# Four layers on 16 images: layers 2 and 3 of one pair of images issued in steps between the tap streams of the next pair, and score rows by ScalarE alone

## The chip, the core and the metric

The kernel runs on one core of a Trainium2 chip. Five engines have each their own queue of instructions: PE (TensorE, matrix products), DVE (VectorE), ACT (ScalarE), POOL (GpSimd) and SP (SyncE, which issues DMAs). The metric is the device time of one execution in microseconds (us), taken as a median of several runs. A profile is one more execution with a hardware record of every instruction; its span goes from the first to the last instruction.

## The reference, cut to what matters

The input x is 16 images of 128 channels and 28 x 28 pixels, in fp32. Four layers follow one another.

```python
# layer 0: group normalization, then x + L1 distances of every 3x3 patch to 128 filters
neg_l1 = -sum(abs(W[f, k] - patch[k]))           # k over 128 channels x 9 taps
# layer 1: two 3x3 convolutions, 4-bit weights, two of nine taps masked; result in 16 levels
out = act_quant(bn(conv(act_quant(bn(conv(x, wq1))), wq2)) + x)
# layer 2, over 784 tokens of 128 channels, on layer-normalized tokens:
Wi = B @ W.T
scores[i, j] = sum_d v[d] * tanh(Wi[j, d] + Wi[i, d])
C = softmax(scores) @ B                          # then 2 of 8 experts for each token
# layer 3: linear attention with elu(.)+1 and a causal mask, then a spectral layer:
# 16 filters, plus and minus, causal convolution over the tokens and a 128x128 mix of each
```

Each layer adds its result to its input. The dear ones are layer 0 (128 x 9 taps of |w - x| over a whole image) and the scores (784 x 784 tanh of 128 channels, of which the symmetric half is computed).

## The kernel before, in words

The kernel has two phases, `conv_layers` (layers 0 and 1, in 8 pairs of images) and `token_layers` (layers 2 and 3, image by image). The levels of all images are kept on chip between them.

**Phase one.** Channels lie on the partitions, and a pair of images is one tile `pad` of 128 x 60 x 30. For each filter and tap one instruction makes a tile `d` of 128 x 1568: ACT takes |x - w| (L312), or DVE takes max(x, w) (L314). |w - x| is 2 max(x, w) - x - w, so a maximum needs the plain tap subtracted, which a matmul with ones does for all filters at once (L304), and a constant `sw`. A second maximum can be added into the same `d` by one more DVE instruction (L316), which saves a tile for PE. PE sums `d` over the channels (L321): a matmul with a column of `sel` into 32 output columns, four filters side by side, in four chunks of 392 pixels. A "stream" is four tiles, one for each quarter of the filters; `in_turn` lays out 264 streams for a pair, with turns that mix ACT tiles and DVE tiles. After each stream one step of `rest` is issued: the quantized convolutions of the pair before, then the group normalization of the pair after. `d` has 16 buffers, `pad` two. At the end of a pair DVE writes `x1p` (L330).

**Phase two.** For every block of 112 tokens, `scores` makes 15 units. DVE adds a column of `wi` to a row of 394 tokens, eight rows to a unit (L709), ACT takes the tanh of the whole tile (L710, 3152 elements), and PE sums over the channels with `vz` (L685), one unit later. `written` moves a block's scores into `sc` after the next block's last unit. After each unit, `tick` issues steps of three generators at fractional rates: `attend` of the image before, then `head` of the next image and experts, linear attention and `normed` of the one before, and `spectral` of the image two before. A spectral job is four matmuls of `up` with a band (L978), a copy by ACT (L984), and a mix into an accumulator (L956); a band is fetched by DMA for two jobs (L963), and the mixing matrices stay on chip. PSUM has two banks for scores, two for accumulators and four that all other steps rotate through. The weights of the spectral layer and its bands are prepared in the steps of image 0.

PE's instructions are kept in the order in which they are written (`in_traced_order`); the other engines' order is set by the tile scheduler near to the written one. Every queue is in order.

Of the kernel before, what the change touches and what calls it, by code (L numbers as in the profile page):

```python
# [9 lines left out]
U8 = mybir.dt.uint8  # L10
# [13 lines left out]
MAX_TAPS, EITHER = [1, 3, 4, 5, 7], 8  # L24
COMMON = [("a", (0,)), ("m", (4,)), ("a", (2,)), ("m", (5,)), ("a", (6,)), ("m", (7,)), ("a", (8,)), ("m", (1, 3))]
FOURTH = [("a", (0,)), ("m", (4,)), ("m", (1,)), ("a", (2,)), ("m", (5,)), ("m", (3,)), ("a", (6,)), ("m", (7,)), ("m", (8,))]


def in_turn():


    quarters = []
    for j, turn in enumerate((0, 2, 5, 7)):
        mine = [(m, *x) for m in range(32) for x in (FOURTH if (m + j) % 4 == 3 else COMMON)]
        quarters.append(mine[turn:] + mine[:turn])
    return list(zip(*quarters))


STREAMS = in_turn()
# [18 lines left out]
class Steps:  # L58


    def __init__(self, *gens, rate=1.0):
        self.gens = [g for g in gens if g is not None]
        self.rate, self.due = rate, 0.0

    def step(self, n=1):
        while n and self.gens:
            try:
                next(self.gens[0])
                n -= 1
            except StopIteration:  # L70
                self.gens.pop(0)

    def tick(self):
        self.due += self.rate
        while self.due >= 1.0:
            self.due -= 1.0
            self.step()

    def each(self):
        while self.gens:  # L80
            self.step()
            yield

    def drain(self):
        while self.gens:
            self.step()
# [8 lines left out]
def rows_of(ap, n):  # L95

    return ap.unsqueeze(0).to_broadcast([n, ap.shape[0]])

# [15 lines left out]
@with_exitstack  # L114
def kernel(ctx: ExitStack, tc: tile.TileContext, a: dict, out: bass.AP):
    nc = tc.nc
    keep = ctx.enter_context(tc.tile_pool(name="keep", bufs=1))

    ident = keep.tile([P, P], F32, name="ident")
    make_identity(nc, ident)  # L120
    ones = keep.tile([P, P], F32, name="ones")
    nc.vector.memset(ones, 1.0)
    mhalf = keep.tile([P, NK], F32, name="mhalf")
    nc.vector.memset(mhalf, -0.5)

    levels = keep.tile([P, B, T], U8, name="levels")

    conv_layers(tc, a, levels, ident, ones, mhalf)
    token_layers(tc, a, out, levels, ident, ones, mhalf)
    in_traced_order(tc, (mybir.EngineType.PE,))  # L130


def rsqrt(nc, out, x, eps, mhalf):

    nc.vector.tensor_scalar(out, x, eps, None, ALU.add)
    nc.gpsimd.tensor_tensor(out, out, mhalf, ALU.pow)  # L136

@with_exitstack  # L140
def conv_layers(ctx, tc, a, levels, ident, ones, mhalf):
    nc = tc.nc
    const = ctx.enter_context(tc.tile_pool(name="a_const", bufs=1))
    xpool = ctx.enter_context(tc.tile_pool(name="a_x", bufs=2))
    small = ctx.enter_context(tc.tile_pool(name="a_small", bufs=2))
    ring = ctx.enter_context(tc.tile_pool(name="a_ring", bufs=16))
    ypool = ctx.enter_context(tc.tile_pool(name="a_y", bufs=3))
    psacc = ctx.enter_context(tc.tile_pool(name="a_acc", bufs=1, space=PSUM))
    psm = ctx.enter_context(tc.tile_pool(name="a_psm", bufs=4, space=PSUM))
    NP = B // 2  # L150

    def load_x(p):
        x = xpool.tile([P, 2, T], F32, tag="x", name=f"x{p}")
        nc.sync.dma_start(x, a["x"][2 * p : 2 * p + 2].rearrange("b c t -> c b t"))
        return x

    xs = {0: load_x(0)}
    w0 = const.tile([P, 9, P], F32, name="w0")
    nc.scalar.dma_start(w0, a["L0_conv_W"])
    wq = {}  # L160
    for name in ("L1_conv_w1", "L1_conv_w2"):
        wq[name] = const.tile([P, 9, P], F32, name=name)
        nc.scalar.dma_start(wq[name], a[name])
# [21 lines left out]
    pads = [const.tile([P, PR, PC], F32, name=f"pad{i}") for i in range(2)]  # L185
    x1p = const.tile([P, PR, PC], F32, name="x1p")
    q1p = const.tile([P, PR, PC], F32, name="q1p")
    for t in (*pads, x1p, q1p):
        nc.vector.memset(t, 0.0)

    nw0 = const.tile([P, 9, P], F32, name="nw0")
    nc.scalar.mul(nw0, w0, -1.0)
# [5 lines left out]
    background = [(k, ones) for k in MAX_TAPS] + [(EITHER, fourth)]  # L198

    wsum = const.tile([P, P], F32, name="wsum")  # L200
    nc.vector.tensor_tensor(wsum, w0[:, EITHER, :], fourth, ALU.mult)
    for k in MAX_TAPS:
        nc.vector.tensor_tensor(wsum, wsum, w0[:, k, :], ALU.add)
    sw_ps = psm.tile([P, 512], F32, tag="psm", name="sw_ps")
    nc.tensor.matmul(sw_ps[:, :1], wsum, ones[:, :1], start=True, stop=True)
    sw = const.tile([P, 1], F32, name="sw")
    nc.vector.tensor_copy(sw, sw_ps[:, :1])

    def quantized_weights():

        for name, w in wq.items():
            nc.scalar.activation(w, w, AF.Tanh)
            yield
            mx = small.tile([P, 1], F32, tag="mx", name="mx_" + name)
            nc.vector.tensor_reduce(mx, w.rearrange("p k f -> p (k f)"), AX.X, ALU.max, apply_absolute_value=True)
            mall = small.tile([P, 1], F32, tag="mall", name="mall_" + name)
            nc.gpsimd.partition_all_reduce(mall, mx, P, bass_isa.ReduceOp.max)
            for _ in range(8):
                yield
            nc.vector.tensor_scalar(mall, mall, 2.0, None, ALU.mult)  # L220
            nc.vector.reciprocal(mx, mall)
            yield
# [4 lines left out]
            yield  # L227


    bn = {}  # L230

    def norms():
        for i, unit in ((0, NLEV), (1, NLEV * NLEV)):
# [3 lines left out]
            for _ in range(4):  # L237
                yield
# [6 lines left out]
            yield  # L245
# [13 lines left out]


    def group_norm(p, lag):
        x, pad = xs[p], pads[p % 2]
        stats = small.tile([P, 2, 2, 6], F32, tag="stats", name=f"stats{p}")
        mv = small.tile([P, 2, 2], F32, tag="mv", name=f"mv{p}")
        for im in range(2):
            for h in range(2):
                nc.vector.bn_stats(stats[:, im, h, :], x[:, im, h * NCK : (h + 1) * NCK])
            nc.vector.bn_aggr(mv[:, im, :], stats[:, im])
            yield
        ps = psm.tile([P, 512], F32, tag="psm", name=f"gm_ps{p}")  # L270
        nc.tensor.matmul(ps[:, :2], grp, mv[:, :, 0], start=True, stop=True)
        for _ in range(lag):
            yield
        gm = small.tile([P, 2], F32, tag="gm", name=f"gm{p}")
        nc.vector.tensor_copy(gm, ps[:, :2])
        dev = small.tile([P, 2], F32, tag="dev", name=f"dev{p}")
# [3 lines left out]
        yield  # L280
        ps = psm.tile([P, 512], F32, tag="psm", name=f"gv_ps{p}")
        nc.tensor.matmul(ps[:, :2], grp, dev, start=True, stop=True)
        for _ in range(lag):
            yield
        rstd = small.tile([P, 2], F32, tag="rstd", name=f"rstd{p}")
        rsqrt(nc, rstd, ps[:, :2], 1e-5, mhalf[:, :2])
        for _ in range(lag):
            yield
        for im in range(2):
# [4 lines left out]
            yield  # L294

    def l1_distances(p, rest):


        pad = pads[p % 2]
        accs = [psacc.tile([P, 512], F32, tag=f"acc{c}", name=f"acc{p}_{c}") for c in range(4)]  # L300

        for i, (k, of) in enumerate(background):
            for c in range(4):
                nc.tensor.matmul(accs[c][:, :NCK], of, window(pad, k, 14 * c, 14), start=i == 0, stop=False)  # L304
        for n, stream in enumerate(STREAMS):
            made = []
            for j, (m, kind, taps) in enumerate(stream):
                f = 32 * j + m
                d = ring.tile([P, 2 * HW, HW], F32, tag="d", name=f"d{p}_{f}_{taps[0]}")
                k = taps[0]  # L310
                if kind == "a":
                    nc.scalar.activation(d, window(pad, k, 0, 2 * HW), AF.Abs, bias=nw0[:, k, f : f + 1])  # L312
                else:
                    nc.vector.tensor_scalar(d, window(pad, k, 0, 2 * HW), w0[:, k, f : f + 1], None, ALU.max)  # L314
                    for k in taps[1:]:
                        nc.vector.scalar_tensor_tensor(  # L316
                            d, window(pad, k, 0, 2 * HW), w0[:, k, f : f + 1], d, ALU.max, ALU.add)
                made.append(d)
            for c in range(4):
                for j, (m, kind, _) in enumerate(stream):  # L320
                    nc.tensor.matmul(  # L321
                        accs[c][32 * j : 32 * j + 32, :NCK], sel[kind][:, 31 - m : 63 - m],
                        made[j][:, 14 * c : 14 * c + 14, :], start=False, stop=n == len(STREAMS) - 1,
                    )
# [723 lines left out]
```

## Time and profile before

| | us |
|---|---|
| median of 3 runs (12472.03 to 12472.23) | 12472.12 |
| profiled execution, its own time | 12472.97 |
| its span | 12470.9 |
| PE busy | 11890.7 (95%) |
| DVE busy | 11408.4 (91%) |
| ACT busy | 10934.1 (88%) |
| phase one, start to the last `x1p` | 0 to 6191 |
| between the phases and image 0 | 6191 to 6753 |
| images with all three generators | 6753 to 11521 |
| the last 366 us, after image 15's scores | 12105 to 12471 |

In the list of groups a line shows the line of the kernel, the engine, the operation, what it writes and reads with partitions x elements, the count, then the total busy time and the mean ns of one, and last the idle time of the engine just before them with what ended it. A matmul in fp32 has two records. Instructions of one engine overlap a little, so a mean is longer than the distance from one start to the next. In a timeline, a line is a start, a length and how many instructions of a group follow each other.

### The profile page before, as it was taken

Reading aid. Unit: us, or ns where it says so; the run is one execution under the profiler, and the core shown is the slowest. Engines: PE = TensorE matmul, PEld = TensorE weight load, DVE = VectorE, ACT = ScalarE, POOL = GpSimd, SP = SyncE. Lnnn points to the kernel's source line nnn. Section 1 sums busy time; section 2 is a strip of 40 time slices with the busy share of each in tenths; the row PEclk is TensorE's granted clock in tenths of the full one; section 3 lists DMA queues with packets and bytes.
Section 4 is the critical chain, followed back from the end, with each engine's and each line's share of the span. In section 5 each row is a group of like instructions: output and inputs, shape, how many; then the busy total and the mean of one; then the engine's idle time right before and its main releaser. Section 6 shows DMA issues by size and latency. Waiting matters only on the chain.

```text
span 12470.9 us, 260867 instructions
## 1 busy us (share of the span) xinstructions
PE 11890.7 (95%) x109746; PEld 5640.7 (45%) x109746; DVE 11408.4 (91%) x23240; ACT 10934.1 (88%) x7253; POOL 294.4 (2%) x129
## 2 busy tenths in 40 slices
PE   9999999999999999999956899999999999999999
PEld 4444444444444444444412444454444454444456
DVE  9989989899998999989989999999999999999982
ACT  8989989899898999989878888888888888888872
POOL 0000000000000000000010000000000000000000
PEclk9999999999999999999989999999999999999999
DMA  0000000000000000000020000000000000000001
GB/s 12 2 4 2 4 1 2 4 2 4 2 2 4 2 4 2 2 1 2 3 75 1 13 19 20 20 20 20 20 20 19 20 20 20 20 19 20 19 24 36
DMA packets 111864, 156.91 MB, mean 13 GB/s; under 512 B 13096, under 2 KB 106208, under 8 KB 110688
## 3 DMA queue, kind: packets, MB, share of 16 engines
q1 hardware_dynamic: 110256, 138.46, 4.1%
q8 instruction: 860, 14.09, 0.5%
q14 instruction: 316, 2.59, 0.1%
q10 hardware_dynamic: 432, 1.77, 0.0%
HBM read 127.34 MB, written 12.85 MB: 11 GB/s over the span
## 4 chain that ended last, share of the span: by engine, by line
PE 57%; DVE 32%; issue 5%; ACT 4%; POOL 1%; DMA 0%; SPq 0%; DVEq 0%; POOLq 0%; ACTq 0%
DVE d L314 19%; PE acc L321 17%; PE sp L685 14%; PE u L978 11%; DVE d L316 5%; DVE th L709 5%; PE acc L956 5%; ACT th L710 3%; PE conv_ps L338 2%; PE av L772 2%; PE ex L843 1%; PE acc L304 1%; ACT d L312 1%; PE acc L947 1%; POOL rs_l L136 1%
## 5 line engine op out<-in xcount | busy, mean ns | idle before, releaser
L312 ACT ACTIVATE d<-pad,nw 128x1568 f32<-128x1568 f32 x3840 | 5781.3, 1622 | 214.6 <-PE acc L321 200.8
L321 PE MATMUL acc<-d,sel_m 128*32 128x392 f32 x36864 | 5148.7, 493 | 66.1 <-DVE d L316 57.2
L710 ACT ACTIVATE th<-th 128x3152 f32<-128x3152 f32 (+1 forms) x1680 | 4475.5, 2688 | 431.7 <-DVE th L709 372.9
L321 PE MATMUL acc<-d,sel_a 128*32 128x392 f32 x30720 | 4737.9, 493 | 21.4 <-ACT d L312 20.5
L709 DVE TENSOR_SCALAR th<-wi 128x394 f32<-128x394 f32 (+1 forms) x12544 | 4437.3, 419 | 244.8 <-PE sp L685 219.5
L314 DVE TENSOR_SCALAR d<-pad,w 128x1568 f32<-128x1568 f32 x4608 | 4430.9, 1029 | 80.6 <-PE acc L321 80.1
L685 PE MATMUL sp<-th,vz 128*32 128x394 f32 (+1 forms) x25088 | 2440.7, 509 | 395.5 <-ACT th L710 395.3
L321 PEld LDWEIGHTS acc<-d,sel_m 128*32 128x32 f32 x36864 | 1980.9, 110 | 1745.2 <-issue 1260.4
L321 PEld LDWEIGHTS acc<-d,sel_a 128*32 128x32 f32 x30720 | 1755.6, 110 | 1522.0 <-issue 1269.9
L978 PE MATMUL u<-band,up 128*128 128x392 f32 (+3 forms) x8192 | 1711.2, 349 | 0.0
L978 PEld LDWEIGHTS u<-band,up 128*128 128x128 f32 x8192 | 1342.4, 190 | 773.0 <-PE sp L685 158.5
L685 PEld LDWEIGHTS sp<-th,vz 128*32 128x32 f32 x25088 | 664.0, 110 | 1833.8 <-issue 797.9
L316 DVE SCALAR_TENSOR_TENSOR d<-pad,w,d 128x1568 f32<-128x1568 f32 x768 | 1417.9, 1846 | 8.7
L984 ACT COPY u<-u 128x392 f32<-128x392 f32 x1024 | 493.1, 482 | 518.6 <-PE u L978 518.4
L956 PE MATMUL acc<-u,m_even 128*128 128x392 f32 x1024 | 463.2, 534 | 0.0
L956 PE MATMUL acc<-u,m_odd 128*128 128x392 f32 (+1 forms) x1024 | 461.7, 533 | 0.0
L849 DVE SCALAR_TENSOR_TENSOR t<-ex,gate,t 128x128 f32<-128x128 f32 x896 | 306.8, 343 | 11.9 <-PE ex L843 10.4
L843 PE MATMUL ex<-ew,xt 128*128 128x512 f32 x448 | 213.9, 600 | 0.4 <-DVE t L849 0.4
L772 PEld LDWEIGHTS av<-n,sc 128*128 128x128 f32 x1568 | 181.8, 191 | 50.1 <-issue 28.2
L772 PE MATMUL av<-n,sc 128*128 128x129 f32 x1568 | 196.2, 279 | 0.0
L956 PEld LDWEIGHTS acc<-u,m_odd 128*128 128x128 f32 x1024 | 155.7, 192 | 10.9 <-issue 10.1
L992 DVE TENSOR_TENSOR y<-acc,mask 128x392 f32<-128x392 f32 x32 | 19.0, 594 | 151.5 <-PE acc L956 151.5
(247 smaller groups left out, 4184.3 us busy)
## 6 DMA issues: line engine op xcount, KB each, us to landing
band<-band SPq DMA_DIRECT2D x512, 196.0 KB
x<-in_x_dram SPq DMA_DIRECT2D x8, 784.0 KB
band<-band_out SPq DMA_DIRECT2D x32, 196.0 KB
out_dram<-y SPq DMA_DIRECT2D x16, 392.0 KB
band_in<-in_L_ffn_phi_dram SPq DMA_DIRECT2D x16, 300.1 KB
m_plus<-in_L_ffn_M_phi_plus_dram SPq DMA_DIRECT2D x32, 128.0 KB
m_minus<-n_L_ffn_M_phi_minus_dram SPq DMA_DIRECT2D x32, 128.0 KB
band_in<-in_L_ffn_phi_dram SPq DMA_DIRECT2D x16, 84.8 KB
```

Of the source, the lines that this page charges most:

```text
L312: nc.scalar.activation(d, window(pad, k, 0, 2 * HW), AF.Abs, bias=nw0[:, k, f : f + 1])
L314: nc.vector.tensor_scalar(d, window(pad, k, 0, 2 * HW), w0[:, k, f : f + 1], None, ALU.max)
L316: nc.vector.scalar_tensor_tensor(d, window(pad, k, 0, 2 * HW), w0[:, k, f : f + 1], d, ALU.max, ALU.add)
L321: nc.tensor.matmul(accs[c][32 * j : 32 * j + 32, :NCK], sel[kind][:, 31 - m : 63 - m], made[j][:, 14 * c : 14 * c + 14, :], start=False, s ...
L685: nc.tensor.matmul(sp[32 * j : 32 * j + 32, lo : lo + w], vz[:, 31 - m : 63 - m], th[:, 4 * k + j, :], start=m == 0, stop=m == Q - 1, skip ...
L709: nc.vector.tensor_scalar(th[:, 4 * k + j, :], wi[:, lo : lo + w], wi[:, i : i + 1], None, ALU.add)
L710: nc.scalar.activation(th, th, AF.Tanh)
L772: nc.tensor.matmul(q[:, i * (P + 1) : (i + 1) * (P + 1)], blk(sc[:, k, :], i0 + i), n1[:, k, :], start=k == 0, stop=k == NT - 1)
L843: nc.tensor.matmul(qs[h], blk(xt, i), ew[:, 4 * h : 4 * h + 4, :], start=True, stop=True)
L956: nc.tensor.matmul(acc[to][:, lag:TH], (m_odd if odd else m_even)[:, k, :], u[:, : TH - lag], start=False, stop=k == NK - 1 and odd == 1)
L978: nc.tensor.matmul(q[:, P * i : TH], up[:, jobs[n][2], i, :], t[:, :w], start=i == 0, stop=i == 3)
L984: nc.scalar.copy(u, held_[n - 1][0][:, :TH])
```

## The change

One set of pools and one loop take the place of the two phases.

- Pair 0 keeps the old taps (`ALONE`, 264 streams). Pairs 1 to 7 use `BESIDE`: 208 streams, more merged second taps on DVE, fewer taps on ACT, seven plain taps.
- Between the streams of pair p, three lanes issue steps: the convolutions of pair p-1, the chain (head, attend, experts, linear attention, normed) and the spectral jobs. A step is of kind `EV` (ACT, DVE, POOL) or `PE`; in a stream the EV steps come ahead of the sums and the PE steps behind them.
- Score units come at two a stream (L689): each of a unit's four rows is one ACT tanh with the column as bias. After the last pair (`alone`) DVE adds and ACT takes the tanh of four rows at once (L682, L684).
- `d` tiles have 10 buffers, rows 14; there is one `pad`. PSUM has four banks for the taps, and one each for scores, spectral output, the chain (`psx`) and jobs with convolutions (`psu`).
- Mixing matrices, quantized convolution weights, expert weights and x for the residual are fetched again by DMA when they are needed. Weights and bands are prepared in pair 0.

```diff
+ALONE = Plan(
+    "alone", [tiles("a:0", "m:4", "a:2", "m:5", "a:6", "m:7", "a:8", "m:13")] * 3
+    + [tiles("a:0", "m:4", "m:1", "a:2", "m:5", "m:3", "a:6", "m:7", "m:8")], (0, 2, 5, 7),
+    [(1, "all"), (3, "all"), (4, "all"), (5, "all"), (7, "all"), (8, "fourth")])
+BESIDE = Plan(
+    "beside", [tiles("m:13", "a:0", "m:45", "m:6", "a:2", "m:78")] * 2
+    + [tiles("m:13", "a:0", "m:7", "m:45", "a:2", "m:8", "m:6"),
+       tiles("m:13", "a:0", "m:7", "a:2", "m:45", "a:6", "m:8")], (0, 2, 4, 5),
+    [(1, "all"), (3, "all"), (4, "all"), (5, "all"), (7, "all"), (8, "all"), (6, "rest")])
+RING, ROWS = 10, 14
+RATE_X, RATE_Y, RATE_S, RATE_C, RATE_A, RATE_0 = 1.2, 0.85, 2.0, 1.0, 1.5, 1.2
...
+class Lane:
+    def run(self, turn):
+        while self.gens:
+            if self.turn is None:
+                self.turn = next(self.gens[0], None)
+                if self.turn is None:
+                    self.gens.pop(0)
+            elif self.turn != turn or (turn == PE and self.other and self.other.holds):
+                return False
+            else:
+                self.turn = next(self.gens[0], None)
+                self.holds = turn == PE
+                if self.turn is None:
+                    self.gens.pop(0)
+                return True
+        return False
...
-                        nc.vector.tensor_scalar(th[:, 4 * k + j, :], wi[:, lo : lo + w], wi[:, i : i + 1], None, ALU.add)
-                nc.scalar.activation(th, th, AF.Tanh)
+                    rows = [rows_pool.tile([P, WIN], F32, tag="row", name=f"row{b}_{i + Q * j}") for j in range(4)]
+                    for j in range(4):
+                        nc.scalar.activation(rows[j], wi[:, i + Q * j : i + Q * j + WIN], AF.Tanh,
+                                             bias=wi[:, i + Q * j : i + Q * j + 1])
+                products.append(lambda sp=sp, ib=ib, m=m, rows=rows: products_of(sp, ib, m, rows))
+                yield
+            while products:
+                products.pop(0)()
...
+            for n in [*mine, None]:
+                yield PE
+                if n is not None:
+                    _, k, odd = jobs[n]
+                    fetch(n + 2)
+                    t, m = got.pop(n)
+                    q = small(f"u{b}_{n}")
+                    for i in range(4):
+                        w = TH - P * i
+                        nc.tensor.matmul(q[:, P * i : TH], up[:, to ^ odd, i, :], t[:, :w], start=i == 0, stop=i == 3)
+                if before is not None:
+                    u, m0, lag = before
+                    nc.tensor.matmul(acc[:, lag:TH], m0, u[:, : TH - lag], start=False, stop=n is None)
+                if n is not None:
+                    yield EV
+                    u = two.tile([P, TH], F32, tag="u", name=f"us{b}_{n}")
+                    nc.scalar.copy(u, q[:, :TH])
+                    before = u, m, odd and (to ^ odd)
...
+        taps_of(0)
+        for n in range(len(streams)):
+            if n == len(streams) - 60 and p + 1 < NP:
+                convs.add(group_norm(p + 1))
+            if n == len(streams) - 8:
+                xr = load_pair(p, f"xr{p}")
+                if p + 1 < NP:
+                    xn = load_pair(p + 1, f"xn{p + 1}")
+            rows(RATE_S if p else 0.0)
+            if n + 1 < len(streams):
+                taps_of(n + 1)
+            ns = ahead()
+            sums(n)
+            raw_taps(1)
+            while products:
+                products.pop(0)()
+            behind(ns)
+        if p + 1 < NP:
+            while convs.gens:
+                whole(RATE_S)
+            pad_pair(p + 1, xn)
...
+    convs.add(quantized_convs(NP - 1))
+    state_of["alone"] = True
+    convs.rate, conv_out.rate = 1.0, 0.5
+    while convs.gens or chain.gens or conv_out.gens or units:
+        whole(1.5 if units else 0.0)
```

`taps_of` issues a stream's four tiles, `sums` its 16 matmuls, `raw_taps` one plain tap; `rows` issues score units; `ahead` runs the lanes' EV steps and `behind` their PE steps; `whole` is a stream without taps.

## The prediction

> **What bounds the kernel now.** I read the busy times of the two phases first, then the groups of instructions, then short stretches of the timeline, since a group's mean is a latency and not the step from one instruction to the next. Phase one (pairs) and the steady part of phase two (images), in the view of busy time by stretch:
>
> ```profile
> 764.00:6191.00 5427.00, 5352.33 (x60309) 2374.90 (x60300) 5136.01 (x5013) 5092.62 (x3415) 4.14 (x6) 1.00 0.01 2
> 6753.00:11521.00 4768.00, 4557.30 (x32725) 2285.48 (x32725) 4431.03 (x14067) 4114.21 (x2652) 209.33 (x53) 1.00 0.07 19
> ```
>
> The columns are length, PE, PEld, DVE, ACT, POOL, clock, DMA. Seven pairs took 5,427 us, 775 us each; 13 images took 4,768 us, 367 us each. No engine has room: PE 99% and 96%, DVE 95% and 93%, ACT 94% and 86%. The groups behind it:
>
> ```profile
> L312 ACT ACTIVATE d<-pad,nw 128x1568 f32<-128x1568 f32 x3840 | 5781.3, 1622 | 214.6 <-PE acc L321 200.8
> L321 PE MATMUL acc<-d,sel_m 128*32 128x392 f32 x36864 | 5148.7, 493 | 66.1 <-DVE d L316 57.2
> L314 DVE TENSOR_SCALAR d<-pad,w 128x1568 f32<-128x1568 f32 x4608 | 4430.9, 1029 | 80.6 <-PE acc L321 80.1
> L316 DVE SCALAR_TENSOR_TENSOR d<-pad,w,d 128x1568 f32<-128x1568 f32 x768 | 1417.9, 1846 | 8.7
> L984 ACT COPY u<-u 128x392 f32<-128x392 f32 x1024 | 493.1, 482 | 518.6 <-PE u L978 518.4
> ```
>
> And the steps, from the timeline (start, length, group, count):
>
> ```profile
> 2998.80 16.64 ACT L312 ACTIVATE d<-pad,nw 128x1568 f32<-128x1568 f32 x11
> 4591.05 6.71 DVE L314 TENSOR_SCALAR d<-pad,w 128x1568 f32<-128x1568 f32 x7
> 4597.68 1.84 DVE L316 SCALAR_TENSOR_TENSOR d<-pad,w,d 128x1568 f32<-128x1568 f32 x1
> 4599.44 3.87 DVE L314 TENSOR_SCALAR d<-pad,w 128x1568 f32<-128x1568 f32 x4
> 7389.98 2.34 ACT L764 ACTIVATE sc<-sc,nowhere 128x448 f32<-128x448 f32 x4
> 7402.65 1.96 ACT L764 ACTIVATE sc<-sc,nowhere 128x336 f32<-128x336 f32 x4
> 8404.70 0.91 PE L956 MATMUL acc<-u,m_odd 128*128 128x392 f32 x2
> 8405.54 1.53 PE L685 MATMUL sp<-th,vz 128*32 128x394 f32 x16
> 8407.00 0.49 PE L896 MATMUL nu<-vx,at 128*128 128x129 f32 x2
> 8410.95 2.85 PE L685 MATMUL sp<-th,vz 128*32 128x394 f32 x32
> 12382.32 1.62 PE L978 MATMUL u<-band,up 128*128 128x392 f32 x8
> 12384.54 1.62 PE L978 MATMUL u<-band,up 128*128 128x392 f32 x8
> ```
>
> Steps: an ACT tap (16.64-1.62)/10 = 1.50 us. A DVE tap (6.71-1.03)/6 = 0.945; a merged second tap 4599.44-4597.68 = 1.76. Four 32-column matmuls run side by side, 32 records in 2.85 us: a round of four is 0.33, a stream of 16 matmuls (two records each) eight rounds, 2.62. A spectral job is 2.22. Between 32-column and full-width work PE loses time: 0.84 for a pair of passes that takes 0.65, then 1.46 for four rounds that take 1.31. That is 0.33 for going over and back.
>
> With these, before: a pair on PE is 264 x 2.62 + 16 (plain taps) + 37 (convolutions) = 745, of 775. An image on PE is 130 (products) + 142 (64 jobs) + 62 (rest) + 105 x 0.33 (going over) = 369, against 367 measured. So phase two is PE end to end, and phase one PE with 4% of stalls. The lone ends (first image 450 us, last transition) make up the rest.
>
> **The change, part by part.** Counts are from the order in which the changed program issues on each engine.
>
> *Taps, pairs 1 to 7.* 208 streams for 264, 288 ACT taps for 480, 544 single DVE taps for 576, 320 merged second taps for 96. Per pair: PE -56 x 2.62 = -147; ACT -192 x 1.50 = -288; DVE -32 x 0.945 + 224 x 1.76 = +364. The seventh plain tap adds 2.6 to PE.
>
> *Rows.* In those pairs a score unit is four ACT rows of 394 with a column as bias, and no DVE add. No row of 394 stands in the trace; the nearest is the exp with a bias column, L764: (2.34-0.66)/3 = 0.56 at 448 elements and (1.96-0.57)/3 = 0.46 at 336. So 0.51 at 394, 402 us an image for 784 rows; the unsplit tanh took 4,475.5/16 = 280. The Trainium skill speaks against it here ("Perfetto Trace Analysis", Optimizing Scalar/DVE Operations: group into larger operations when the engine is saturated) and prices an instruction at about 93 ns on ScalarE. By that, with the slope of the two exp rows, 0.83 ns, a row would be 0.42 and a pair's rows 605; by the exp row they are 740. I take the row. Ends: 0.42, and 0.63 if nothing overlaps.
>
> *Sum of a full pair (2 to 7).* It carries some 360 units and 115 spectral jobs (1.8 images).
> - PE: 546 taps + 18 plain + 37 convolutions + 247 products + 255 jobs + 111 rest = 1,214 (mean of the six 1,225); going over and back once a stream 208 x 0.33 = 69. 1,290.
> - ACT: 432 + 740 + 42 (copies) + 32 = 1,246.
> - DVE: 514 + 566 + 154 (normalization, experts, softmax, convolutions) = 1,234.
> All three are level, 6 us a stream. The old kernel would need 775 + 1.8 x 367 = 1,436 for that work. That is also the point of indifference below.
>
> *Stalls.* The level sums hide uneven streams: one with three merged tiles costs DVE 8.1 us, one with none 2.8. Taking the busiest engine in each stretch of k streams, the going over included, and adding up, a pair is 1,463 (k=2), 1,409 (4), 1,378 (8), 1,348 (26). The same sums for a pair before are 821 (4), 790 (8), 749 (16), measured 775 with 16 tap tiles, four streams of slack; for an image 371 at 15 steps, measured 367. The changed kernel has 10 tap tiles (2.5 streams), 14 rows (1.75 streams), and one PSUM bank each for scores, chain and jobs. Shorter slack, shorter stretch: I take the mean of 4 and 8, 1,393, plus 7 at the border of two pairs, where the single pad, x1p and accs leave PE without work (before, DVE's wait at that border was 1.95). 1,400.
>
> *Single banks.* A second rule speaks against the change (same page, Matmuls: independent groups should rotate through PSUM banks, so that evacuation overlaps the next group). By the rule a job would take 1.48 plus the copy, 0.48, plus the hand-overs, about 2.2 without its mix, 2.9 with it: +80 a pair. By the row the copy fits beside the previous job's mix (jobs start 2.22 apart, the mix is 0.74 of it), so 0 with a free ACT. In a stream the copy stands behind rows and taps on ACT and has a stream's length to come. I take 0, and keep 80 for the range. The score bank adds a wait of its own: `written` on DVE (13 times a pair) needs the block's last products, and behind it in DVE's queue stand taps, for which PE's next sums wait. The built order has put taps of the same stream ahead of it, which cover it; uncovered it is some 2 us each, 26 a pair.
>
> *Moved: first pair.* Weights, bands and constants leave the start of phase two, where the first two images took 450 each, and go to pair 0. DVE there: 264 streams 714 + 43 = 757; bands wait for their DMA on PE in the same stream (16 of them; between 0 and 3.9 us each, the length such DMA pieces have in the chain), merged weights hold ring tiles. With 2.5 streams of slack (783 at k=4): 850 (800 to 920).
>
> *Moved: spectral DMA.* Each job now fetches its own band (196 KB) and its matrix (64 KB), 2,048 issues for 512. SP holds them until a buffer is free; each is issued two jobs ahead, 12 us in pairs, 4.4 in the tail. Band pages moved 19 GB/s at 7% DMA share. Cover for it: the two jobs; without it some 2 us a job.
>
> *Pair 1.* DVE leads with 1,166; rows start late. 1,283 by the same stretches and border.
>
> *Tail.* 662 units (3.4 images) and 320 jobs stay behind. PE: 1,453 + 440 steps x 0.33 = 1,598. The three full images are 992 + 130, over 0.96 for DVE's wait on the single score bank at each of seven blocks: 1,168. Ahead of them 140; behind them the last image's chain with the jobs of image 14, 240 (before: 215, from 12,105 to 12,320), and 150 for the last 64 jobs. 1,700.
>
> **Sum.** Start 22 + pair 0 850 + pair 1 1,283 + 6 x 1,400 + tail 1,700 = 12,255. The profiled execution was 12,472.97 with a span of 12,470.9, and the median of the runs is 12,472.12, so 2 us lie around the span: 12,257. I say 12,260, 1.7% faster. 0.2%, 25 us, is about what a measurement here can tell from no change.
>
> **Rivals.**
> - *Lockstep (slower).* PE runs in written order and ends each stream with chain and job steps that need what DVE and ACT do at the end of the same stream; one bank each means the next step can't start early. Then slack is one stream and k=2 holds: 1,463 + 8. With pair 0 at 900, pair 1 at 1,326 and a tail of 1,780: 12,850. For it: the stream sums of 2.8 and 8.1 us. Against: taps are written one stream ahead. It decides from 1,436 a pair, 0.17 us a stream above my value.
> - *Near-full overlap.* k=26: 1,356 a pair, 800, 1,258, tail 1,630: 11,850. For it: phase two ran PE at its sum. Against: it had four score tiles and four banks for a 3.5 us step.
> - *Row price.* At 0.63 ACT is 1,246 + 1,440 x 0.12 = 1,419 and alone the bound; with 5% stalls 1,490 a pair, 12,800.
>
> **How the numbers follow.** Likeliest 0.45 (its own range 12,080 to 12,450; 0.36 faster, 0.05 same, 0.04 slower). Overlap 0.24, faster. Lockstep 0.25 and row price 0.06, slower but for 0.02 each of faster and same. Faster 0.62, same 0.07, slower 0.31. The range 11,800 to 12,880 leaves out the outer part of overlap and of lockstep.
>
> **What would show it.** Borders of pairs 2 to 7 (x1p writes) 1,400 us apart; PE busiest, its waits short and shared between DVE taps and ACT rows; row steps of 0.51; 2.62 a stream of taps; jobs some 6 us apart. Wrong: row steps above 0.60, PE waiting for the same-stream step of chain or jobs, or a tail over 1,850.

## The result, and the profile after

| | us |
|---|---|
| before, median of 4 runs (12471.80 to 12472.23) | 12472.08 |
| after, median of 4 runs (12368.58 to 12381.23) | 12373.18 |
| ratio, 95% interval | 0.9921, 0.9904 to 0.9939 |
| profiled execution of the changed kernel, its span | 12366.9 |

The change makes the kernel 0.8% faster, 99 us. The forecast was 1.7%, 212 us: the direction and the range hold, the size does not. The `x1p` writes divide the span into the stages of the forecast sum:

| stage | forecast | measured | difference |
|---|---|---|---|
| start and pair 0 | 22 + 850 | 957 | +85 |
| pair 1 | 1,283 | 1,280 | -3 |
| pairs 2 to 7 | 6 x 1,400 | 6 x 1,393 = 8,356 | -44 |
| tail | 1,700 | 1,774 | +74 |
| sum | 12,255 | 12,367 | +112 |

Where the interleaving runs in full, in pairs 2 to 7, the time came within 44 us of the forecast sum. The miss lies in the two stages at the ends.

Busy time by stretch of the changed kernel, in the four stages (length, PE, PEld, DVE, ACT, POOL, granted clock of TensorE as a share of full speed, DMA share, GB/s):

```profile
0.00:957.00 957.00, 832.16 (x8558) 316.89 (x8562) 820.83 (x1007) 751.68 (x516) 52.48 (x58) 0.98 0.12 35
957.00:2237.00 1280.00, 1080.05 (x9582) 394.63 (x9574) 1172.67 (x1181) 1072.73 (x1526) 9.09 (x6) 0.97 0.01 5
2237.00:10596.00 8359.00, 7964.02 (x69853) 3601.37 (x69854) 7496.35 (x8788) 7602.50 (x11611) 93.33 (x60) 0.99 0.10 28
10596.00:12367.00 1771.00, 1598.64 (x10168) 840.04 (x10166) 1234.60 (x3857) 1160.36 (x1140) 24.82 (x20) 0.97 0.20 53
```

In pairs 2 to 7 PE is busy 95% of the time, ACT 91% and DVE 90%: 1,327, 1,267 and 1,249 us a pair, where the sum had 1,290, 1,246 and 1,234. In pair 0 no engine is above 87%, and in the tail PE is at 90%. That is where to look for lost time.

The groups of the changed kernel that answer to those of before:

```profile
L689 ACT ACTIVATE row<-wi 128x394 f32<-128x394 f32 x9904 | 5291.4, 628 | 231.6 <-PE sp L672 230.0
L1088 PE MATMUL acc<-d,sel_m 128*32 128x392 f32 x35072 | 5104.8, 505 | 187.6 <-DVE d L1103 178.0
L1101 DVE TENSOR_SCALAR d<-pad,w 128x1568 f32<-128x1568 f32 x4384 | 4352.2, 1032 | 508.2 <-PE acc L1088 499.9
L1099 ACT ACTIVATE d<-pad,w 128x1568 f32<-128x1568 f32 x2496 | 3927.7, 1610 | 600.5 <-PE acc L1088 570.6
L1103 DVE SCALAR_TENSOR_TENSOR d<-pad,w,d 128x1568 f32<-128x1568 f32 x2336 | 4260.2, 1846 | 6.9
```

The tap instructions cost what they cost before (1,032, 1,610 and 1,846 ns a piece). What is new is their idle time: 508 us on DVE and 600 us on ACT wait for a PE sum to give a tap tile back (before: 81 and 215), and ACT's rows wait 232 us for the products to give a row tile back. PE in turn is idle for 188 us ahead of its sums, nearly all of it for a merged tap of DVE. All three engines take turns at being late, as one would expect of a level schedule with short buffers.

The timeline of the changed kernel (start, length, group, count, and the wait ahead of it) has the new step, the row:

```profile
4004.43 4.23 ACT L689 ACTIVATE row<-wi 128x394 f32<-128x394 f32 x8
```

(4.23 - 0.628) / 7 = 0.515 us from row to row.

### The profile page after: what moved, and what is told of

Its sections match the earlier page's. It is cut to its first block, busy times and chain, and to the rows that moved or that the text cites. A ratio compares the mean times of both kernels' runs of the same rounds, so it can differ in the third digit from the quotient of the medians.

```text
span 12366.9 us, 236560 instructions
## 1 busy us (share of the span) xinstructions
PE 11474.9 (93%) x98156; PEld 5152.9 (42%) x98156; DVE 10724.4 (87%) x14828; ACT 10587.3 (86%) x14792; POOL 179.7 (1%) x144
## 5 line engine op out<-in xcount | busy, mean ns | idle before, releaser
L689 ACT ACTIVATE row<-wi 128x394 f32<-128x394 f32 x9904 | 5291.4, 628 | 231.6 <-PE sp L672 230.0
L1101 DVE TENSOR_SCALAR d<-pad,w 128x1568 f32<-128x1568 f32 x4384 | 4352.2, 1032 | 508.2 <-PE acc L1088 499.9
L1099 ACT ACTIVATE d<-pad,w 128x1568 f32<-128x1568 f32 x2496 | 3927.7, 1610 | 600.5 <-PE acc L1088 570.6
L1103 DVE SCALAR_TENSOR_TENSOR d<-pad,w,d 128x1568 f32<-128x1568 f32 x2336 | 4260.2, 1846 | 6.9
L672 PE MATMUL sp<-row,vz 128*32 128x394 f32 x19808 | 2107.1, 495 | 0.7 <-ACT row L689 0.7
L672 PEld LDWEIGHTS sp<-row,vz 128*32 128x32 f32 x19808 | 735.7, 110 | 1073.8 <-issue 784.0
L684 ACT ACTIVATE th<-th 128x1576 f32<-128x1576 f32 x660 | 968.2, 1519 | 174.4 <-DVE th L682 149.0
L682 DVE TENSOR_SCALAR th<-wi 128x394 f32<-128x394 f32 x2640 | 924.1, 423 | 39.5 <-PE sp L672 39.2
L984 PE MATMUL out<-us,mat 128*128 128x392 f32 (+1 forms) x2048 | 929.3, 536 | 0.0
L672 PE MATMUL sp<-th,vz 128*32 128x394 f32 x5280 | 517.1, 507 | 36.0 <-ACT th L684 35.7
L672 PEld LDWEIGHTS sp<-th,vz 128*32 128x32 f32 x5280 | 139.0, 110 | 326.2 <-issue 190.3
```

Source lines behind the costliest of these rows:

```text
L672: nc.tensor.matmul(sp[32 * j : 32 * j + 32, lo : lo + WIN], vz[:, 32 - m : 64 - m], rows[j], start=False, stop=m == Q - 1, skip_group_chec ...
L682: nc.vector.tensor_scalar(th[:, j, :], wi[:, i + Q * j : i + Q * j + WIN], wi[:, i + Q * j : i + Q * j + 1], None, ALU.add)
L684: nc.scalar.activation(th, th, AF.Tanh)
L689: nc.scalar.activation(rows[j], wi[:, i + Q * j : i + Q * j + WIN], AF.Tanh, bias=wi[:, i + Q * j : i + Q * j + 1])
L984: nc.tensor.matmul(acc[:, lag:TH], m0, u[:, : TH - lag], start=False, stop=n is None)
L1103: nc.vector.scalar_tensor_tensor(d, window(pad, k, 0, 2 * HW), w0[:, k, f : f + 1], d, ALU.max, ALU.add)
```

## The experiments

Each kernel is the changed one with the edit shown; `...` stands for lines left out. The times of stages are read from its `x1p` writes and its span. Ten of the kernels ran once, the last two four times. Stages that an edit leaves alone came out at 952 to 957 us (pair 0), 1,392 to 1,395 (a full pair) and 1,763 to 1,776 (tail), so smaller differences than these mean nothing.

**Pair 0: what the preparation costs.** Three edits. The first leaves the preparation of bands and mixing matrices out. (`slot` takes a tile from the ring of tap tiles; 16 loads bring two bands each, and each of the 32 bands is one matmul.)

```diff
-            t = slot(2 * TH, f"band_in{r}").rearrange("p (k t) -> p k t", k=2)
...
-                nc.tensor.matmul(q[:, :TH], flip, t[:, k, :], start=True, stop=True)
...
-                nc.scalar.copy(o, q[:, :TH])
...
+            nc.sync.dma_start(band[r], w0.rearrange("p k f -> p (k f)")[:, :TH])
...
+            nc.sync.dma_start(mats_ar[j], w0[:, j, :])
+        for k in range(2 * NK):
+            nc.sync.dma_start(mats[k], w0[:, k % 9, :])
```

> Leaves out the preparation of bands and mixing matrices in pair 0 (pieces of the layer-0 weights are copied in their place; the later work is unchanged). Theory P (the preparation's steps between the streams cost the excess of pair 0): the first x1p write comes down from 957 us to about 820, which is 22 + 264 streams at the 3.02 us they take after 600 us. Rival R (10 tap tiles in place of 16 are the cause, whatever the steps do): it stays above 900. Rest of the kernel as it was, so the whole time is about 12,235 by P and above 12,310 by R.

Measured: pair 0 ends at 836 instead of 957 (-121), and the kernel takes 12,240.1 us; the full pairs are as they were, the tail is 10 us shorter. So the preparation is the larger part of the excess of pair 0.

The second keeps all of that work, and puts its inputs into tiles that are idle in pair 0 instead of the ring of tap tiles:

```diff
-            t = slot(2 * TH, f"band_in{r}").rearrange("p (k t) -> p k t", k=2)
+            t = idle(2 * TH, r // 2, f"band_in{r}").rearrange("p (k t) -> p k t", k=2)
...
-            t = slot(NS * P, f"m_ar_in{j}").rearrange("p (s e) -> p s e", s=NS)
+            t = idle(NS * P, j, f"m_ar_in{j}").rearrange("p (s e) -> p s e", s=NS)
...
```

> Same work; the inputs of bands and matrices are loaded into tiles that are idle in pair 0 and no longer into tap tiles, so that all 10 tap tiles serve the taps. If the preparation costs by the tap tiles that it holds: first x1p write at 870 us or earlier. If it costs by waits in the queues (PE for a band's DMA, DVE for a matrix's DMA, copies) it stays at 930 or later. My guess is 890, both.

Here `idle` rotates over the tiles `tt`, `wi`, `up` and `dg` of the token layers.

Measured: 909 (-48), 12,306.2 us, between the two forecasts. The third spreads the same steps thinner over the streams:

```diff
-RATE_0 = 1.2
+RATE_0 = 0.65
```

> The chain's rate in pair 0 is 0.65 steps a stream in place of 1.2, so that the preparation is spread over nearly all of the pair. If the excess comes from a crowd of steps in the first 550 us (each stream can hide some): first x1p write at 890 to 910. If each step costs a fixed wait: it stays at 945 to 965.

Measured: 950, 2 us under the lowest of the kernels with an unchanged pair 0; 12,377.7 us. So it is not crowding: the cost goes with the step and not with the distance between steps.

PE's waits in pair 0 of the changed kernel (waiting line, releaser: us in all, times, longest):

```profile
PE acc L1088 <- DVE d L1103: 41.8, 33, 3.6
PE band L482 <- DMA band_in<-in_L_ffn_phi_dram: 26.5, 14, 2.6
```

The same with the inputs in idle tiles:

```profile
PE acc L1098 <- DVE d L1113: 42.1, 36, 2.8
...
PE band L492 <- ACT band_out L495: 1.7, 3, 0.6
```

The wait for the band's DMA is gone when the DMA no longer waits for a tap tile. The 121 us are thus 48 for tap tiles held and 73 that stay when no tap tile is held. The records of the tap sums, 32 to a stream, say where. Bands are made from 178 to 327 us, matrices from 338 to 533. From 150 to 350 us the changed kernel makes 1,520 records and the kernel without preparation 2,174; from 350 to 550 us they make 1,531 and 2,176. At 2.93 us a stream the bands thus cost 60 us and the matrices 59. With the inputs in idle tiles the same count gives 34 and 34. The tap tiles held are 25 us of each half. In the half of the bands PE shows them as its own wait (26.5 less 1.7); in the half of the matrices no wait of PE for a DMA shows them.

Busy time by stretch of the kernel without preparation says what work was added:

```profile
0.00:836.00 836.00, 764.03 (x8494) 310.27 (x8498) 768.17 (x803) 734.36 (x484) 40.22 (x42) 1.00 0.07 22
```

Against the first row above, DVE is busy for 53 us more with 204 more instructions, the mixing of the matrices. PE is busy for 68 us more, but only 32 of these are matmuls of bands; the same tap sums (8,434 records in both kernels) are busy for 781 us instead of 742. A stretch of 100 us in which it runs, busy time of the changed kernel:

```profile
200.00:300.00 100.00, 78.84 (x693) 25.94 (x696) 55.18 (x52) 64.27 (x57) 6.09 (x10) 0.94 0.27 81
```

and the same stretch without preparation:

```profile
200.00:300.00 100.00, 93.95 (x1080) 37.88 (x1084) 93.28 (x87) 93.76 (x62) 0.00 (x0) 1.00 0.01 2
```

PE, DVE and ACT all lose, by 15 to 38 of 100 us. That fits in-order queues in which the work of all three stands behind a late preparation step; where each stood was not followed one by one.

**Pair 0 and the pairs: slack.** Without the bands and matrices, pair 0 still takes 836 - 22 = 814 us, 3.08 us a stream, where the same streams took 742 before. One difference is the ring: 10 tap tiles for 16. Stretches of 150 us without preparation, the tap sums alone (length, PE, PEld, clock, DMA share, GB/s), show what it does. First the changed kernel with 10 tap tiles, then the runs below with 11 and with 13, last the kernel before with 16:

```profile
550.00:700.00 150.00, 143.02 (x1642) 56.44 (x1634) 1.00 0.01 2
600.00:750.00 150.00, 146.28 (x1730) 61.34 (x1722) 1.00 0.02 7
550.00:700.00 150.00, 148.20 (x1768) 72.83 (x1764) 1.00 0.02 7
550.00:700.00 150.00, 147.37 (x1766) 65.85 (x1762) 1.00 0.01 2
```

At 32 records a stream these are 2.92, 2.77, 2.71 and 2.72 us: 13 tiles run at the pace of 16. For 264 streams the step from 16 to 10 is some 53 of the 72 us. The rest lies mostly in the first 150 us, where the kernel without bands and matrices makes 1,062 such records and the kernel before 1,280; the constants of the token layers, which the change moved there, are made in that time. Tiles are scarce, so a tap tile was paid for with four row tiles, in two runs:

```diff
-RING, ROWS = 10, 14
+RING, ROWS = 10, 10      # second run: 11, 10
```

> 10 row tiles in place of 14 (1.25 streams in place of 1.75). If slack decides the stalls of a full pair (mine: stretches of some 6 streams at the present slack): pairs 2 to 7 go from 1,393 to about 1,410 each. If rows never wait for long because PE frees them in the same stream: unchanged within 4.

> 11 tap tiles, 10 row tiles (the room of one tap tile taken from rows). To be read beside the run with 10 and 10. If tap tiles are the short slack: a full pair 15 us or more under that run, and pair 0 20 us or more under 935. If neither matters: within 4 us a pair.

Measured: with 10 rows pairs 2 to 7 take 1,406 us each for 1,393, and the kernel 12,448.8. That is +13, where the forecast was +17; it is +18 in pairs 2 to 5 alone. The eleventh tap tile then takes 40 us off pair 0 (956 to 917), as forecast for a short slack, but only 5 off each full pair, where 15 or more were forecast; the kernel takes 12,379.8 us. So the room of one tap tile serves the pairs better as four row tiles (13 us for 5) and pair 0 better as a tap tile, and at this size the two cancel.

**The tail: which single bank.** The forecast put the tail's stalls down to DVE's wait on the one score bank. In the tail the banks of the taps stand empty. Three kernels give them to the scores, to the chain, and to both:

```diff
# the scores, in the tail: two of the tap banks in turn
+            if alone():
+                sp = psacc.tile([P, 512], F32, tag=f"acc{ib % 2}", name=f"sp{b}_{ib}")
...
# the chain, in the tail: rotates over its own bank and two of the tap banks
     def ps(name):
+        if state_of["alone"]:
+            turn_of["ps"] += 1
+            if turn_of["ps"] % 3:
+                return psacc.tile([P, 512], F32, tag=f"acc{1 + turn_of['ps'] % 3}", name=name)
```

> Only the scores take two of the free banks in turn in the tail; the chain stays on its single bank. All banks together brought the tail from 1,771 to 1,682. If the wait at the border of two score blocks was the cost (my prediction's step: DVE's wait on the single score bank at each of seven blocks): about 1,690. If the chain's single bank was the cost: 1,750 or more.

> Only the chain's steps rotate through three banks in the tail; scores stay on their single bank. The counterpart: about 1,690 if the chain's bank was the cost, 1,750 or more if the score bank was. If both shares add up, the two savings of e4 and e5 make 89 us together.

> In the tail the four banks of the taps are free; scores take two of them in turn, the chain's steps the other two in turn with their own. Theory B (single banks make the tail's image 416 us where its work on PE is 374): an image takes about 388, tail 1,771 to about 1,680. Rival L (each image has a stretch of experts and attention steps that is bound by its own chain of waits, banks or not): 405 to 416 an image, tail above 1,730. Pairs unchanged.

Measured: scores alone 12,353.8 us (tail 1,756, -18), chain alone 12,291.0 (1,691, -83), both 12,286.0 (1,685, -89). It is the chain's bank. The 18 us of the score bank are hardly more than the spread of an unchanged tail. PE's waits in the tail, of the changed kernel:

```profile
PE ex L842 <- DVE t L846: 40.6, 25, 1.7
PE sp L672 <- ACT th L684: 35.7, 41, 2.3
```

with more score banks:

```profile
PE ex L845 <- DVE t L849: 40.6, 25, 1.7
PE sp L672 <- ACT th L687: 37.8, 43, 2.3
```

and with more chain banks:

```profile
PE sp L679 <- ACT th L691: 54.6, 64, 3.1
PE sp L675 <- DVE sc L709: 9.8, 7, 1.5
```

The matmul of the experts, `ex` (four experts to a bank), waits 25 times, 1.6 us each, for DVE to empty the bank of the four before, and the rest of PE's queue stands behind it. One such place of the changed kernel, from the timeline:

```profile
11256.75 1.10 PE L842 MATMUL ex<-ew,xt 128*128 128x512 f32 x2 [1.56 <-DVE t L846]
11257.77 1.53 PE L672 MATMUL sp<-th,vz 128*32 128x394 f32 x16
```

The last tanh ahead of these score products (ACT L684) ended at 11,256.2, so here they were ready before the wait ended; it was not followed at the other places. Score banks leave the wait of `ex` at the same 40.6 us; chain banks remove it. This names half of the 83; the rest is spread over the shorter waits of the chain, the longest of them 10 us in all. Score products then wait somewhat more (35.7 to 54.6): the next limit is the tanh.

**Are both parts of the change needed?** Two kernels keep the interleaving and take one part back each: rows by DVE adds and a common tanh (the four rows then lie in a tap tile), and the old taps in all pairs (with the rate of units per stream scaled to 264 streams).

```diff
# DVE adds, one tanh of four rows, in the pairs too
-                if alone():
+                if True:
```

```diff
# old taps in all pairs
-        plan = BESIDE if p else ALONE
+        plan = ALONE
...
-            rows(RATE_S if p else 0.0)
+            rows(RATE_S * 208 / 264 if p else 0.0)
```

> Score rows in the pairs as before the change and as in the tail: DVE adds the column to four rows, ACT takes one tanh over them; steps and taps as in the changed kernel. DVE of a full pair comes to 1,705 us (373 units x 4 x 0.324 more), ACT to 1,013: a pair takes 1,760 to 1,860, the whole about 15,100. If the interleaving alone carried the change, a pair would stay under 1,450.

> All pairs with the 264 streams of the old taps, score units at the same number a pair (1.58 a stream); rows by ACT as in the changed kernel. A full pair: ACT 1,572, PE 1,409 + 264 x 0.33 = 1,496, DVE 877. ACT leads: 1,620 to 1,680 a pair, a tail shorter by its 100 units (about 1,550), the whole about 13,900. If PE alone set the pair, 1,500 to 1,550 a pair.

Measured: 14,748.6 us with DVE adds (forecast about 15,100), and 13,766.3 with the old taps (forecast about 13,900). Busy time by stretch in pairs 2 to 7, with DVE adds:

```profile
2546.00:12985.00 10439.00, 8840.38 (x69826) 3629.97 (x69822) 10331.65 (x17484) 6334.75 (x5080) 138.19 (x60) 0.95 0.08 23
```

and with the old taps:

```profile
2447.00:12306.00 9859.00, 9317.61 (x82078) 4138.09 (x82074) 5494.27 (x7758) 9528.62 (x13211) 78.20 (x63) 0.99 0.09 26
```

Either way one engine becomes the bound: DVE at 99%, 1,740 us a pair (a little under the forecast), or ACT at 97%, 1,643 us a pair. (The old taps' longer pairs carry more rows, 10,384 for 9,904, so their tail is shorter, 1,459 us for a forecast of 1,550.) With one of the two shifts taken back, the interleaved kernel is 18% or 10% slower than the kernel before. So neither the shift of taps to DVE nor the shift of rows to ACT pays alone. Both taken back at once was not run; the sums of the two expectations then give an estimate of 1,496 us for PE, 1,339 for ACT (1,572 less 1,246 - 1,013) and 1,348 for DVE (877 plus 1,705 - 1,234), so PE alone would need more than the 1,436 of the kernel before. The new split without interleaving was not run either.

**A faster version.** Idle tiles for the preparation and all banks in the tail, together:

> The first two edits of the run with a shared ring, without the shared ring: 12,373 - 48 - 89 = 12,236 if they add up, and 0.981 of the kernel before.

Measured: 12,234.2 us (12,232.9 to 12,237.2), 0.9809 of before (0.9792 to 0.9825), 1.1% under the changed kernel. Pair 0 ends at 908, pairs 2 to 7 are unchanged at 1,394, the tail is 1,684: the two gains add up. A third edit on top takes rows and taps from one ring of 13 tiles, a unit of four rows in one tile:

```diff
-RING, ROWS = 10, 14
+RING, ROWS = 13, 0
...
-                    rows = [rows_pool.tile([P, WIN], F32, tag="row", name=f"row{b}_{i + Q * j}") for j in range(4)]
+                    th = slot(4 * WIN, f"row{b}_{ib}_{m}").rearrange("p (a b) -> p a b", b=WIN)
+                    rows = [th[:, j, :] for j in range(4)]
```

> Three edits together: preparation through idle tiles, free banks in the tail, and one ring of 13 tiles for taps and for the four rows of a unit in place of 10 tap tiles and 14 rows. The first two are worth 48 and 89 (their single runs): 12,235. The shared ring gives pair 0 all 13 tiles, another 40 or more (11 tiles gave 40), and a full pair some slack, 0 to 20 each: 12,080 to 12,200. If a unit's tile, freed only as a whole, costs more slack than it gives: above 12,240.

Measured: 12,380.5 us (ratio 0.9928, 0.9913 to 0.9942), a miss of 180 to 300 us: the other case that was named beforehand, above 12,240, came. Pair 0 did gain, 908 to 863, but a full pair went from 1,394 to 1,426. PE's waits in pairs 2 to 7, first of the changed kernel:

```profile
PE acc L1088 <- DVE d L1103: 74.3, 62, 2.8
PE ex L842 <- DVE t L846: 40.3, 28, 3.3
PE u L981 <- ACT us L988: 36.8, 42, 2.5
```

and then with one ring:

```profile
PE acc L1106 <- DVE d L1121: 154.5, 127, 4.9
PE u L1001 <- ACT us L1008: 47.8, 55, 2.2
```

PE's wait for merged taps doubles; the other two hardly move (`ex` waits 46.3 us with one ring). A unit's tile comes free only when its fourth row is used, so that DVE's taps stand behind rows: this would fit, but it was not tried apart.

## Why the forecast had the direction right and the gain too large

- *Taps and rows of a full pair: right; the sums a little short.* A row costs 0.515 us for the forecast 0.51. The rule of the Trainium skill that the prediction weighed against it ("Perfetto Trace Analysis", Optimizing Scalar/DVE Operations: about 93 ns an instruction, so 0.42 us) would have put ACT at 1,111 us in a pair, where it measured 1,267. (The two exp rows shown give a slope of 0.86 ns an element and not the 0.83 that the prediction took; with 0.86 the rule gives 0.43 and 1,130, which changes nothing.)
- *Stalls by stretches: the size right, in part by luck.* Pairs took 1,393 us for 1,400, but PE was busy for 1,327 of them, for a sum of 1,290, and idle for 66, for 110: two errors that nearly cancel. That slack counts is shown (four row tiles fewer, 13 us a pair). But of the 394 us that PE waits in the six pairs, 100 are for taps, 0.7 for rows and 234 for steps of the chain. The prediction listed a wait for such steps among its signs of being wrong and gave the chain no term of its own. Whether more banks for the chain would shorten these waits in the pairs was not tried; there the taps hold the four banks. Lockstep (1,463) and near-full overlap (1,356) did not come; a pair stayed 43 us under the point of indifference at 1,436.
- *Single banks of jobs: near the 0 of the forecast in the pairs.* PE's wait of a job for its copy is 36.8 us in six pairs, 6 us a pair, of the 80 kept for the range. *Spectral DMA: hidden.* Bands land a median 2.4 us after their issue, and none of PE's waits in the pairs is for a band.
- *Pair 0: mis-sized, 850 for 935.* The step "With 2.5 streams of slack (783 at k=4): 850" failed in two terms. It laid 67 us for the preparation on top of 783; the preparation costs 121. Its work on DVE is 53 us for 43, the bands' matmuls, 32 us on PE, had no term, and tap tiles held by its inputs, named but not priced, cost 48. PE's wait for the bands' DMA was sized well (26.5 us, 2.6 the longest). The rest of pair 0 takes 814, not 783. There the stretch of four streams held, since at 2.92 us the 264 streams make 771; what had no term lies around them, mostly in the first 150 us.
- *Tail: mis-sized, 1,700 for 1,774, by a step with the wrong cause.* PE's work was right, 1,599 us busy for a sum of 1,598; the waits were not, 172 us for 102. "Over 0.96 for DVE's wait on the single score bank" made 389 us of an image; in the chain that ended last, the same point of two images lies 416 us apart. More score banks gave 18 us back, more chain banks 83. The skill's rule on rotating banks (same page, Matmuls) was weighed for the jobs, where the row spoke against it and the runs agree. For the chain, whose single bank the prediction names, it was not weighed, and that bank was put at nothing without a reason. There DVE's emptying of the bank lies between two matmuls, and 83 us is what the rule was worth.

The two stages make +159 (85 and 74), the pairs take 47 back, and 112 is the whole difference.

## What to carry to other kernels

In this kernel interleaving paid only with the work split anew, so that the engines were level in the mixture. The buffers for slack, a few tiles for each stream of work, set how near to the level sum one comes: ten tap tiles 2.92 us a stream, thirteen 2.71. A rate in an undisturbed stretch, against the number of tiles, shows it better than the time of a stage. Work out the cost of the ends, where the mixture fills and drains, as carefully as the middle: price each preparation step on every engine it touches and in the buffers it holds. When one phase has gone, give its PSUM banks to the dependent chain that is left: here a single bank stopped PE's queue between two matmuls of the chain, for 83 us in the tail.

## What the runs showed that was not expected

- Fewer, larger tiles in a common ring were slower in the pairs than separate small ones (1,426 for 1,394), although any tile could serve either use.
- The granted clock was 0.94 in the stretch of pair 0 in which PE is 79% busy, and 1.00 without the preparation at 94%. No rule follows: it was also 1.00 in the first 50 us of the changed kernel, with PE 41% busy, and from 300 to 350 us of the run with idle tiles, with PE 84% busy. Over pair 0 it was 0.98 for 1.00; if PE had set the pace throughout, that would be 2% of 957 us, 19 us of the 121 (an estimate from above). How much it was was not measured apart.
